# A factorization-machine kernel in fp32 pieces: P5's copy subtracted early from two outputs, P3's halves in two pairs of banks, a split first load, and one more kind of wait on GpSimd

## The chip, the cores and the metric

The kernel runs on one core of a Trainium2 chip. The metric is the device time of one execution in microseconds. Before the change it is 1290.17 us, the median of three runs (1287.72, 1290.17 and 1290.63).

## The reference

x is 1024 x 512, weight 64 x 512 x 512 (embedding, feature, model), lin_w 512 x 512, all float32:

```python
out_lin = x @ lin_w.T + lin_b
xv = jnp.einsum('bf,efm->bem', x, weight)
zp = jnp.einsum('bf,efm->bem', jnp.square(x), jnp.square(weight))
interaction = 0.5 * jnp.sum(jnp.square(xv) - zp, axis=1)
return out_lin + interaction
```

Nearly all the work is xv: 1024 x 512 times 512 x 32768, squared and summed over the 64 embeddings. zp needs only the sum over e of the squared weights, so it is one 512 x 512 product, as the linear layer is.

## The kernel before, in words

**One product in seven parts.** Every 2 x 2 block product is made from seven block products, P1 to P7, in Strassen's manner. x is cut into four blocks (A11, A12, A21, A22) and their sums R5, R6, R7, R3. The weights come in 32 slices `h`, each of four blocks `w11`, `w12`, `w21`, `w22` of 128 x 2 x 512 and sums of them in `T`, which GpSimd's accumulating DMAs make. In every slice the parts run in the order `(1, 6, 2, 3, 7, 5, 4)`, where 5 is that of the next slice.

**fp32 in three pieces.** Each operand is split into pieces H, L and K in the type fp32r; one part is then H times H, L times L and, some matmuls later, K times K (`product`, line 695; two 128 x 512 matmuls for each of H, L and K and each of the four row groups). ScalarE makes H by a scaled copy (line 359), VectorE or GpSimd makes L, GpSimd makes the K of the weights (line 377). The pieces of x (`X1H` to `X7K`) are made once, in `x_pieces`. For x blocks marked "DMA" in `X_SPLIT`, ScalarE writes three scaled copies and two accumulating DMAs, issued by GpSimd, finish L and K; for those marked DVE, VectorE does it in two instructions. The first slice's P1 and P2 are plain fp32 matmuls, as are the linear layer (lines 509 and 520) and the squares (line 520); a plain 128 x 512 matmul has two records in the trace.

**Banks.** PSUM is used as four tiles `bank_0` to `bank_3`, each a pair of 128 x 512 banks. The planner treats a read or write of one half of such a pair as a touch of the whole pair.

**Start.** Two zero matmuls (line 537) run while the first loads come in. A11 and A12 are loaded by SP in halves (`load_x`, line 421), lin_w by ScalarE's queue in four pieces of 256 KB (`load_lw`, line 426, tiles `p5_0` and `p5_1`, shown as `p`). The linear layer's seven parts follow; VectorE makes the column sums `lt1` to `lt4` that its P5, P6, P7 and P4 need (line 371, `p<-p,p`) and then the x sums R5, R7, R6 and R3.

**The plan.** The instructions are not issued in the order of the code. `Plan` simulates the engines with a table of costs, orders each engine's list by due times that are counted back from TensorE's chain, does so 60 times with some due times drawn earlier, and keeps the order that ends first. `landing(name, at)` tells it when a load arrives; `key` sets TensorE's order. VectorE instructions with two SBUF inputs are marked `both`, since GpSimd and VectorE hold each other up there; the planner may let a GpSimd instruction wait, by a semaphore (`o.after`), for such a VectorE instruction.

**End.** After the last slice the squares run as seven parts (`one_level`) into four outputs o(r,c), which have been filled with the linear layer (`lind`) and the accumulated interaction (`accd`). `into` adds or subtracts one bank half from an output half on VectorE, `store` sends a half (256 KB) to HBM. o(0,0) is the tile `p1_0`, o(1,0) `p1_1`, o(1,1) `p5_1`, o(0,1) `p5_2`. P1 and P2 make o(0,0). P5 is copied twice by ScalarE, into `z` and `y` (tiles `w`); P6 and P7 are subtracted from these and the result is subtracted from o(0,1) and o(1,1).

Of the kernel before, what the change touches and what calls it, by code (L numbers as in the profile page):

```python
# [14 lines left out]
AF = mybir.ActivationFunctionType  # L15
# [15 lines left out]
X_SPLIT = {5: DVE, 6: DVE, 3: DVE, 7: DVE, 1: "DMA", 2: "DMA", 4: "DMA"}  # L31
# [10 lines left out]
class Plan:  # L42
# [104 lines left out]
    def forward(self, chain):  # L147
# [62 lines left out]
        while len(done) < len(ops):  # L210
            now = heapq.heappop(times)
            moved = True
            while moved:
                moved = False
                for e in pending:
# [40 lines left out]
def kernel(  # L256
# [24 lines left out]
    nc = tc.nc  # L281
# [8 lines left out]
    H = B // 2  # L290
# [141 lines left out]
    load_x("A11", 0, 3.9)  # L432
# [4 lines left out]
    load_lw(nc.scalar, [0, 1], 1, 7.8)  # L437
    load_x("A12", 1, 8.2)
    load_lw(nc.scalar, [2, 3], 1, 8.8)
    for at, (n, k) in enumerate((("A22", 0), ("A22", 1), ("A21", 0), ("A21", 1))):  # L440
        load_x(n, k, 10.0 + 0.8 * at)
    nc.sync.dma_start(bias[:], lin_b)
    landing("bias", 13.5)
# [96 lines left out]
    plan.add({PE: 3.0}, None, (), tuple(f2), key=-2000)  # L540
# [313 lines left out]

    last = wsquare()
# [9 lines left out]
    def into(n, bank, sub, u):  # L865
        o = buf[n][:, u]
        dve(o, o, buf[bank[u]], sub, ((n, u), bank[u]), ((n, u),))

    def store(r, c, u):
        n = o_name[r, c]  # L870
        dma(out_dst[:, 2 * c + u, ts(r, H)], buf[n, u], ((n, u),), (), 1.0, (SP, ACT))

    f1, f2, f3, f4 = four()
    key = slot[0]
    one_level(1, right, left, f1, True, key)
    one_level(2, right, left, f2, True, key + 2.5)
    for u in range(2):
        into(o_name[0, 0], f1, False, u)
        into(o_name[0, 0], f2, False, u)
        store(0, 0, u)  # L880
    one_level(5, right, left, f3, True, key + 5)
    z, y = kept["w"](), kept["w"]()
    for n in (z, y):
        for u in range(2):
            used((n, u), n)
            act(buf[n, u], buf[f3[u]], AF.Copy, (f3[u],), ((n, u),), 512)
# [5 lines left out]
    one_level(4, right, left, f3, True, key + 11)  # L892
    for u in range(2):
        into(o_name[1, 0], f3, False, u)
    one_level(7, right, left, f1, False, key + 14)
    for u in range(2):
        into(y, f1, False, u)
        n = o_name[1, 1]
        dve(buf[n, u], buf[n, u], buf[y, u], True, ((n, u), (y, u)), ((n, u),), 512, True)
        store(1, 1, u)  # L900
        into(o_name[1, 0], f1, False, u)
        store(1, 0, u)
    one_level(3, right, left, f4, True, key + 17)
    for u in range(2):
        into(o_name[0, 1], f4, True, u)
        store(0, 1, u)
# [43 lines left out]
```

## Time and profile before

| what | before |
|---|---|
| median of 3 runs | 1290.17 us (1287.72 to 1290.63) |
| the profiled execution | 1289.52 us |
| its span, first to last instruction | 1286.7 us |
| TensorE busy | 1277.7 us, 99% of the span |
| VectorE, GpSimd, ScalarE busy | 1221.4, 1047.2, 967.5 us |
| mean granted TensorE clock | 0.999 |
| DMA | 172.96 MB, 134 GB/s |

Around the span lie 1289.52 - 1286.7 = 2.8 us in that execution. In the timeline a row is: start in us, length in us, engine, line, operation, output and inputs, shape, count, and in brackets the idle time of the engine before it with the instruction that ended it. Several neighbouring instructions of one kind are merged into a row. The letters behind the tile names (`w`, `p`, `bank`) stand for all tiles of that family.

### The profile page before, as it was taken

To read this page: it belongs to the slowest core of one execution; us is meant where nothing else is said; L and a number is where in the kernel's file an instruction comes from. 1 tells how busy PE (TensorE), PEld (TensorE's weight loads), DVE (VectorE), ACT (ScalarE), POOL (GpSimd) and SP (SyncE) were. 2 spreads that over 40 slices of the span, in tenths; PEclk is the share of its full clock that TensorE was granted. 3 is DMA by queue.
4 is the path that set the end of the run, shared out by engine and by line. 5 is a ranking of instruction groups with operands and counts; after the bars stand their busy time and mean duration, and the time that the engine had idled before them with its cause. 6 is when DMAs were issued, how large, how long until landed. Compare 5 with 4: busy or idle time off the path is not lost.

```text
span 1286.7 us, 15428 instructions
## 1 busy us (share of the span) xinstructions
PE 1277.7 (99%) x5476; PEld 1024.1 (80%) x5476; DVE 1221.4 (95%) x1016; ACT 967.5 (75%) x1009; POOL 1047.2 (81%) x534
## 2 busy tenths in 40 slices
PE   9999999999999999999999999999999999999998
PEld 4688888888888888888888888888888888888883
DVE  6799999999999999999999999999999999999996
ACT  7578777777787777877777877777778777787781
POOL 2879988888898888898888888888889788889881
PEclk9999999999999999999999999999999999999999
DMA  8886654446654455664445665444665444565456
GB/s 239 189 226 148 145 119 120 99 112 152 147 124 123 103 109 141 152 140 119 106 103 131 148 152 116 119 99 112 151 147 129 119 99 109 143 151 137 129 109 162
DMA packets 68348, 172.96 MB, mean 134 GB/s; under 512 B 22960, under 2 KB 23984, under 8 KB 68272
## 3 DMA queue, kind: packets, MB, share of 16 engines
q0 software_dynamic: 20736, 73.93, 33.4%
q1 hardware_dynamic: 45440, 95.18, 22.4%
q10 hardware_dynamic: 2096, 2.88, 0.6%
q8 instruction: 42, 0.69, 0.2%
q14 instruction: 34, 0.28, 0.1%
HBM read 160.43 MB, written 6.29 MB: 130 GB/s over the span
## 4 chain that ended last, share of the span: by engine, by line
PE 98%; DVE 1%; DMA 0%; ACT 0%; DVEq 0%; issue 0%
PE bank L695 94%; PE bank L520 3%; PE bank L509 1%; DVE X7K L365 0%; DVE p L371 0%; DMA p<-lin_wT 0%; DVE bank L365 0%; DVE X3K L365 0%; DVE w L371 0%; DVE w_sum L384 0%; ACT pH L359 0%; DVEq L946 0%; DVEq L371 0%
## 5 line engine op out<-in xcount | busy, mean ns | idle before, releaser
L377 POOL TENSOR_TENSOR pK<-pH,pL 128x1024 fp32r<-128x1024 f32 x222 | 570.5, 2573 | 154.8 <-PE bank L695 150.2
L359 ACT ACTIVATE sq<-bank 128x1024 f32<-128x1024 f32 x256 | 262.0, 1023 | 97.2 <-issue 47.3
L384 DVE TENSOR_REDUCE acc<-sq 128x16 f32<-128x1024 f32 x256 | 309.0, 1208 | 2.6 <-ACT sq L359 2.6
L377 POOL TENSOR_TENSOR pL<-T,pL 128x1024 fp32r<-128x1024 f32 x96 | 255.3, 2660 | 16.2 <-ACT pL L359 16.2
L365 DVE SCALAR_TENSOR_TENSOR bank<-bank,w 128x1024 f32<-128x1024 f32 x192 | 234.6, 1222 | 0.7 <-PE bank L695 0.6
L371 DVE TENSOR_TENSOR w<-bank,p 128x1024 f32<-128x1024 f32 x128 | 155.8, 1217 | 25.9 <-PE bank L695 25.9
L359 ACT ACTIVATE p<-bank 128x1024 f32<-128x1024 f32 x128 | 130.8, 1023 | 58.7 <-PE bank L695 58.5
L365 DVE SCALAR_TENSOR_TENSOR pL<-pH,w 128x1024 fp32r<-128x1024 f32 x62 | 163.1, 2631 | 0.3 <-ACT pH L359 0.3
L365 DVE SCALAR_TENSOR_TENSOR bank<-bank,p 128x1024 f32<-128x1024 f32 x128 | 153.2, 1218 | 6.6 <-ACT p L359 5.7
L359 ACT ACTIVATE pL<-T 128x1024 fp32r<-128x1024 f32 x96 | 101.3, 1055 | 75.8 <-issue 70.1
L377 POOL TENSOR_TENSOR pL<-w,pL 128x1024 fp32r<-128x1024 f32 x64 | 155.0, 2421 | 2.3 <-ACT pL L359 2.3
L384 DVE TENSOR_REDUCE w_sum<-wsq 128x16 f32<-128x1024 f32 x128 | 154.7, 1209 | 2.1 <-ACT wsq L359 2.1
L359 ACT ACTIVATE pH<-w 128x1024 fp32r<-128x1024 f32 x126 | 133.2, 1057 | 10.6 <-PE bank L695 6.4
L359 ACT ACTIVATE wsq<-w 128x1024 f32<-128x1024 f32 x128 | 134.8, 1053 | 5.0 <-DVE w_sum L384 5.0
L396 POOL DMA_DIRECT2D T<-weight x96 | 92.4, 963 | 36.6 <-DMA T<-weight 17.0
L359 ACT ACTIVATE pH<-T 128x1024 fp32r<-128x1024 f32 x96 | 101.2, 1054 | 0.0
L359 ACT ACTIVATE pL<-w 128x1024 fp32r<-128x1024 f32 x64 | 68.1, 1064 | 40.7 <-PE bank L695 23.6
L695 PE MATMUL bank<-pH,X4H 128*128 128x512 f32 x256 | 81.3, 398 | 0.0
L695 PE MATMUL bank<-pL,X4L 128*128 128x512 f32 x256 | 79.5, 392 | 0.0
L695 PE MATMUL bank<-pH,X5H 128*128 128x512 f32 x256 | 79.2, 391 | 0.0
L695 PE MATMUL bank<-pH,X3H 128*128 128x512 f32 x256 | 79.0, 390 | 0.2 <-DVE w L371 0.2
L695 PE MATMUL bank<-pL,X3L 128*128 128x512 f32 x256 | 78.8, 389 | 0.0
(117 smaller groups left out, 2552.4 us busy)
## 6 DMA issues: line engine op xcount, KB each, us to landing
w<-weight SPq DMA_DIRECT2D x128, 512.0 KB, 5.9
T<-weight POOLq DMA_DIRECT2D x96, 512.0 KB, 6.1
T<-weight SPq DMA_DIRECT2D x32, 512.0 KB, 5.0
w<-weight POOLq DMA_DIRECT2D x32, 512.0 KB, 6.5
accd<-turned SPq DMA_DIRECT2D x64, 32.0 KB, 5.7
p<-lind SPq DMA_DIRECT2D x4, 512.0 KB, 4.2
out<-p ACTq DMA_DIRECT2D x7, 256.0 KB, 2.1
w<-xT SPq DMA_DIRECT2D x6, 256.0 KB, 5.1
```

What stands on the lines that cost most here:

```text
L359: nc.scalar.activation(o, i, func, bias=bias, scale=scale)
L365: return nc.vector.scalar_tensor_tensor(o, i, scalar, j, ALU.mult, op)
L371: return (nc.vector.tensor_sub if sub else nc.vector.tensor_add)(o, a, b)
L377: return (nc.gpsimd.tensor_sub if sub else nc.gpsimd.tensor_add)(o, a, b)
L384: lambda _: nc.vector.tensor_reduce(o, i.rearrange("p a (m e) -> p a m e", e=E), axis=AX.X, op=ALU.add),
L396: {POOL: 0.62}, lambda _: nc.gpsimd.dma_start(o, i, accum_op=ALU.add),
L509: return nc.tensor.matmul(buf[bank[u]], b[:, k, ts(u, P)], a[:, k, :], start=first and k == 0, stop=k == KH - 1, skip_group_check=True,)
L520: made = nc.tensor.matmul(buf[bank[u]], b[:, k, ts(u, P)], a[:, k, :], start=first and k == 0, stop=k == KH - 1, skip_group_check=True,)
L695: made = nc.tensor.matmul(buf[bank, j], buf[x][:, k, ts(2 * half + j, P)], buf[w][:, k, :], start=first and k == 0, stop=k == KH - 1, skip ...
```

## The change

Five edits, of which two act through the planner:

1. X1's pieces L and K come from VectorE (`X_SPLIT[1]` is DVE) and no longer from three ScalarE copies and two accumulating DMAs.
2. The planner adds a semaphore wait where GpSimd starts a compute instruction while, by the plan, a `both` instruction of VectorE is running and none is held back. That is the case when VectorE got its turn because GpSimd's next instruction was a DMA issue.
3. The first lin_w load (256 KB) becomes two of 128 KB. The arrival times that the planner is told are changed; the zero matmuls are planned with 3.4 instead of 3.0 us.
4. The squares at the end: P5 is copied once, into `z`, and that copy is subtracted from o(0,1) and o(1,1) at once; P6, P7 and P3 are subtracted from the outputs directly. P2 comes after the last K parts of the last slice (`key + 4` for `key + 2.5`).
5. P3's two halves go to one half each of two pairs (`f3 = f4[0], f2[0]`), before to the two halves of one pair.

```diff
-X_SPLIT = {5: DVE, 6: DVE, 3: DVE, 7: DVE, 1: "DMA", 2: "DMA", 4: "DMA"}
+X_SPLIT = {5: DVE, 6: DVE, 3: DVE, 7: DVE, 1: DVE, 2: "DMA", 4: "DMA"}
...
                     elif tensor and held is None and free[DVE] > now and running[DVE].both:
+                        o.after = running[DVE]
                         ends(e, o, free[DVE] + cost)
...
-    load_lw(nc.scalar, [0, 1], 0, 3.9)
-    load_x("A11", 1, 5.2)
-    load_lw(nc.scalar, [2, 3], 0, 5.6)
+    load_lw(nc.scalar, [0], 0, 4.3)
+    load_lw(nc.scalar, [1], 0, 5.1)
+    load_x("A11", 1, 5.9)
+    load_lw(nc.scalar, [2, 3], 0, 7.0)
...
-    plan.add({PE: 3.0}, None, (), tuple(f2), key=-2000)
+    plan.add({PE: 3.4}, None, (), tuple(f2), key=-2000)
...
+    def columns(n, m, sub, u):
+        o, i = buf[n][:, u], buf[m][:, u]
+        dve(o, o, i, sub, ((n, u), (m, u)), ((n, u),), 512, True)
+
+    v, f2, f5, f4 = four()
+    f3 = f4[0], f2[0]
+    one_level(1, right, left, v, True, key)
+    one_level(2, right, left, f2, True, key + 4)
...
+    one_level(5, right, left, f5, True, key + 6)
+    z = kept["w"]()
+    for u in range(2):
+        used((z, u), z)
+        act(buf[z, u], buf[f5[u]], AF.Copy, (f5[u],), ((z, u),), 512)
+        for r in range(2):
+            columns(o_name[r, 1], z, True, u)
+    one_level(6, right, left, v, False, key + 8)
+    for u in range(2):
+        into(o_name[0, 1], v, True, u)
...
-    one_level(6, right, left, f1, False, key + 8)
-    for u in range(2):
-        into(z, f1, False, u)
-        n = o_name[0, 1]
-        dve(buf[n, u], buf[n, u], buf[z, u], True, ((n, u), (z, u)), ((n, u),), 512, True)
...
-    one_level(3, right, left, f4, True, key + 17)
+    one_level(7, right, left, v, False, key + 14)
     for u in range(2):
-        into(o_name[0, 1], f4, True, u)
+        into(o_name[1, 1], v, True, u)
+        store(1, 1, u)
+        into(o_name[1, 0], v, False, u)
+        store(1, 0, u)
+    one_level(3, right, left, f3, True, key + 17)
+    for u in range(2):
+        into(o_name[0, 1], f3, True, u)
         store(0, 1, u)
```

The lists of the engines are the same from about the fourth slice to the last one; they differ in about the first hundred instructions of VectorE and ScalarE, the first seventy of GpSimd, and at the end. A line number of the kernel after is one to two (at the end four) higher.

The first place is VectorE's list from its first instruction. `p5_0`, `p5_1` hold lin_w, `p1_1` the column sums `lt1` and `lt2`, `p5_2` the sums `lt3` and `lt4`; `sq_0` is R5, `w_0` R7. Before:

```order
L371 TENSOR_TENSOR p1_1_108<-p5_0_111 128x512
L371 TENSOR_TENSOR p1_1_108<-p1_1_108,p5_1_112 128x512
L371 TENSOR_TENSOR p5_2_113<-p5_0_111,p5_1_112 128x512
L371 TENSOR_TENSOR p5_2_113<-p5_1_112,p1_1_108 128x512
L371 TENSOR_TENSOR sq_0_104<-w22_1_92,p1_0_107 128x1024
L371 TENSOR_TENSOR w_0_109<-w11_1_87,p1_0_107 128x1024
```

After:

```order
L372 TENSOR_TENSOR X1L_66<-w11_1_87,X1H_65 128x1024
L372 TENSOR_TENSOR p1_1_108<-p5_0_111 128x512
L372 TENSOR_TENSOR p1_1_108<-p1_1_108,p5_1_112 128x512
L372 TENSOR_TENSOR p5_2_113<-p5_1_112,p1_1_108 128x512
L372 TENSOR_TENSOR p5_2_113<-p5_0_111,p5_1_112 128x512
L366 SCALAR_TENSOR_TENSOR X1K_67<-X1H_65,X1L_66 128x1024
L372 TENSOR_TENSOR sq_0_104<-w22_1_92,p1_0_107 128x1024
```

X1L stands ahead of the column sums and X1K between them and R5; `lt4`, which P4 reads, comes before `lt3`.

The second place is GpSimd's list in the first slice, with the semaphores that each instruction waits for. `pL_0`, `pK_0` belong to P5 of the first slice, `pL_2` to `w22`. Before:

```order
L377 TENSOR_TENSOR pL_0_98<-T_0_93,pL_0_98 128x1024 [waits DMASW0_49,Activation_49]
L396 DMA T_0_93<-weight 128x1024 [waits Activation_49,Pool_49]
L377 TENSOR_TENSOR pK_0_101<-pH_0_95,pL_0_98 128x1024
L396 DMA w12_0_88<-weight 128x1024 [waits DMAHW0_49,Activation_49]
L377 TENSOR_TENSOR pL_2_100<-w22_0_91,pL_2_100 128x1024 [waits DMAHW2_49,Activation_49]
```

After:

```order
L378 TENSOR_TENSOR pL_0_98<-T_0_93,pL_0_98 128x1024 [waits DMASW0_49,DVE_49,Activation_49]
L397 DMA T_0_93<-weight 128x1024 [waits Activation_49,Pool_49]
L378 TENSOR_TENSOR pK_0_101<-pH_0_95,pL_0_98 128x1024 [waits DVE_49]
L397 DMA w12_0_88<-weight 128x1024 [waits DMAHW2_49,Activation_49]
L378 TENSOR_TENSOR pL_2_100<-w22_0_91,pL_2_100 128x1024 [waits DMAHW3_49,DVE_49,Activation_49]
```

The order is the same; the three compute instructions now wait for VectorE: by the plan for X3L, X3K and X7K. These are the only three waits of this kind that are added in the whole program.

The third place is the end of VectorE's list, from the work on P6 on. `bank_0` holds P1, P6 and P7 in turn, `bank_2` P5 and then P4, `bank_3` P3 (after: `bank_3` and `bank_1`); `wsq_0` is the last part of the interaction. Before:

```order
L365 SCALAR_TENSOR_TENSOR p5_1_112<-wsq_0_106,p5_1_112 128x512
L371 TENSOR_TENSOR w_1_110<-w_1_110,bank_0_114 128x512
L371 TENSOR_TENSOR p1_1_108<-p1_1_108,bank_0_114 128x512
L371 TENSOR_TENSOR p5_1_112<-p5_1_112,w_1_110 128x512
L371 TENSOR_TENSOR w_1_110<-w_1_110,bank_0_114 128x512
L371 TENSOR_TENSOR p5_1_112<-p5_1_112,w_1_110 128x512
L371 TENSOR_TENSOR p5_2_113<-p5_2_113,bank_3_117 128x512
L371 TENSOR_TENSOR p1_1_108<-p1_1_108,bank_0_114 128x512
L371 TENSOR_TENSOR p5_2_113<-p5_2_113,bank_3_117 128x512
```

After:

```order
L372 TENSOR_TENSOR p5_2_113<-p5_2_113,w_0_109 128x512
L372 TENSOR_TENSOR p5_2_113<-p5_2_113,bank_0_114 128x512 x2
L372 TENSOR_TENSOR p1_1_108<-p1_1_108,bank_2_116 128x512
L366 SCALAR_TENSOR_TENSOR p5_1_112<-wsq_0_106,p5_1_112 128x512
L372 TENSOR_TENSOR p1_1_108<-p1_1_108,bank_2_116 128x512
L366 SCALAR_TENSOR_TENSOR p5_2_113<-wsq_0_106,p5_2_113 128x512
L372 TENSOR_TENSOR p5_1_112<-p5_1_112,bank_0_114 128x512
L372 TENSOR_TENSOR p1_1_108<-p1_1_108,bank_0_114 128x512
L372 TENSOR_TENSOR p5_1_112<-p5_1_112,bank_0_114 128x512
L372 TENSOR_TENSOR p5_2_113<-p5_2_113,bank_3_117 128x512
L372 TENSOR_TENSOR p1_1_108<-p1_1_108,bank_0_114 128x512
L372 TENSOR_TENSOR p5_2_113<-p5_2_113,bank_1_115 128x512
```

Before, three instructions stand from P3's first half on, and both P3 rows read one pair, whose matmuls end together; after, P3's first half is alone in `bank_3` and one row stands behind the last matmul. The subtraction of the P5 copy (`w_0`) from o(0,1) now stands ahead of the two rows that take P6 out of `bank_0`, into which P7 is accumulated next.

More of the change, by code (lines that the diff above doesn't have):

```diff
@@ L430, in load_lw @@
             landing((n, z % KH, c), at)
-    load_x("A11", 0, 3.9)
-    load_lw(nc.scalar, [0, 1], 0, 3.9)
-    load_x("A11", 1, 5.2)
-    load_lw(nc.scalar, [2, 3], 0, 5.6)
+    load_x("A11", 0, 4.2)
+    load_lw(nc.scalar, [0], 0, 4.3)
+    load_lw(nc.scalar, [1], 0, 5.1)
+    load_x("A11", 1, 5.9)
+    load_lw(nc.scalar, [2, 3], 0, 7.0)
     load_x("A12", 0, 7.4)
-    load_lw(nc.scalar, [0, 1], 1, 7.8)
-    load_x("A12", 1, 8.2)
-    load_lw(nc.scalar, [2, 3], 1, 8.8)
+    load_lw(nc.scalar, [0, 1], 1, 8.8)
+    load_x("A12", 1, 8.5)
+    load_lw(nc.scalar, [2, 3], 1, 9.6)
     for at, (n, k) in enumerate((("A22", 0), ("A22", 1), ("A21", 0), ("A21", 1))):
-        load_x(n, k, 10.0 + 0.8 * at)
+        load_x(n, k, 10.1 + 0.7 * at)
     nc.sync.dma_start(bias[:], lin_b)
-    landing("bias", 13.5)
+    landing("bias", 12.5)
     nc.scalar.preload_act_table(AF.Square)
@@ L853, with into, store @@
                 dma_add(buf[n, u], acc_dram[:, ch, ts(r, H)], acc_names(ch), ((n, u),), 1.4, 5.0)
+    def into(n, bank, sub, u):
+        o = buf[n][:, u]
+        dve(o, o, buf[bank[u]], sub, ((n, u), bank[u]), ((n, u),))
+    def store(r, c, u):
+        n = o_name[r, c]
+        dma(out_dst[:, 2 * c + u, ts(r, H)], buf[n, u], ((n, u),), (), 1.0, (SP, ACT))
+    def columns(n, m, sub, u):
[3 more added lines that the diff above has]
+    f3 = f4[0], f2[0]
+    key = slot[0]
+    one_level(1, right, left, v, True, key)
+    one_level(2, right, left, f2, True, key + 4)
+    for u in range(2):
+        into(o_name[0, 0], v, False, u)
+        into(o_name[0, 0], f2, False, u)
+        store(0, 0, u)
+    one_level(5, right, left, f5, True, key + 6)
[8 more added lines that the diff above has]
+        into(o_name[0, 1], v, True, u)
+    one_level(4, right, left, f5, True, key + 11)
+    for u in range(2):
+        into(o_name[1, 0], f5, False, u)
     last = wsquare()
```

30 lines of the change are left out of this document (removed).

## The prediction

> **What bounds the kernel now.** I read the page first, then TensorE's waits, then three stretches of the timeline: the start, 24 to 44 us, the end.
>
> ```profile
> PE 1277.7 (99%) x5476; PEld 1024.1 (80%) x5476; DVE 1221.4 (95%) x1016; ACT 967.5 (75%) x1009; POOL 1047.2 (81%) x534
> ...
> PE 98%; DVE 1%; DMA 0%; ACT 0%; DVEq 0%; issue 0%
> ```
>
> The first row is the engines' busy time, the second the chain that ended last: 98% of it is TensorE. The stage table says where the rest can lie (length, then TensorE's busy time):
>
> ```profile
> 40.00:1240.00 1200.00, 1199.75 (x5258) 982.44 (x5257) 1158.33 (x951) 923.33 (x960) 1015.48 (x508) 1.00 0.55 130
> ```
>
> In these 1200 us TensorE misses 0.25 us. The change leaves the matmuls and, but for the last few, their order, so it can touch only what TensorE waits for and what lies before its first and behind its last matmul. TensorE's waits, all of them (total, times, longest):
>
> ```profile
> PE bank L695 <- DVE p L371: 1.4, 1, 1.4
> PE bank L537 <- PEq L939: 0.8, 1, 0.8
> PE bank L509 <- DMA p<-lin_wT: 0.6, 1, 0.6
> PE bank L695 <- DVE w L371: 0.2, 1, 0.2
> ```
>
> So there are four small prizes: 0.6 us at the first real matmul, 1.4 us near 38 us, 0.2 us near 1047 us, and the tail. A change of 0.2% is 2.6 us, about what a measurement of this kernel can tell from none; the total is of that size.
>
> **The first load (edit 3).** Zero matmuls, the linear layer, and when the loads land behind their issue (first line ScalarE's lin_w, second SP's x; min, median, max):
>
> ```profile
> 0.74 2.04 ACTq L426 DMA_DIRECT2D p<-lin_wT  x4
> 0.79 3.75 PE L537 MATMUL bank<-const-float32-0.0 128*128 128x512 f32 x4 [0.79 <-PEq L939]
> 5.16 7.13 PE L509 MATMUL bank<-w,p 128*128 128x512 f32 x16 [0.63 <-DMA p<-lin_wT]
> 5.90 1.06 ACT L359 ACTIVATE X1L<-w 128x1024 fp32r<-128x1024 f32 x1 [1.81 <-DMA w<-xT]
> ```
> ```profile
> DMA to landing us min/median/max: 4.4/6.1/7.1
> ```
> ```profile
> DMA to landing us min/median/max: 3.4/5.1/6.4
> ```
>
> The first lin_w piece lands at 0.74 + 4.4 = 5.14, and TensorE starts at 5.16; the first half of A11 is there by 0.75 + 3.4 = 4.15, and the zero matmuls end at 4.54. With half the bytes ahead the first piece lands earlier by the time of 128 KB:
>
> ```profile
> 3.40:4.40 1.00, 1.00 (x2) 0.00 (x0) 0.00 (x0) 0.70 (x1) 0.00 (x0) 1.00 1.04 343
> ```
>
> At 343 GB/s that is 0.38 us alone and 0.76 us where x takes half. So TensorE starts between 4.54 and 4.76, and gains 0.40 to 0.62; I take 0.6. Next late is A11's second half: it lands by 5.90 (ScalarE's wait above) and is wanted after four records of 0.43 us, at 4.54 + 1.72 = 6.26. Then P4 needs the column sums:
>
> ```profile
> 9.53 1.89 DVE L371 TENSOR_TENSOR p<-p,p 128x512 f32<-128x512 f32 x3
> 12.13 3.60 PE L520 MATMUL bank<-w,p 128*128 128x512 f32 x8
> 12.24 1.23 DVE L371 TENSOR_TENSOR sq<-w,p 128x1024 f32<-128x1024 f32 x1 [0.82 <-DMA p<-xT]
> ```
>
> P4 at 12.13 - 0.6 = 11.5 would just meet the sums' end at 11.42; in the new order the sum that it reads is the third of the four, done at 10.8. X1L runs before 8.80, when VectorE was idle. X1K (1.22 us by X6K's row below) falls into the gap of 0.82 us before R5, so R5 ends 0.4 us later, at 13.9; P5 wants it when P4's eight records of 0.43 us are through, near 15.0. Two ScalarE copies and two GpSimd DMA issues leave the early lists; nothing waited for them. Edit 1 costs nothing here while those 1.1 us hold.
>
> **The stall near 38 us (edit 2).** VectorE, GpSimd and TensorE up to 39 us:
>
> ```profile
> 22.52 1.22 DVE L365 SCALAR_TENSOR_TENSOR X6K<-X6H,X6L 128x1024 fp32r<-128x1024 f32 x1
> ...
> 28.87 1.32 DVE L371 TENSOR_TENSOR p<-p,bank 128x512 f32<-128x512 f32 x2
> 30.10 5.72 DVE L365 SCALAR_TENSOR_TENSOR X7K<-X7H,X7L 128x1024 fp32r<-128x1024 f32 x1
> 35.75 0.68 DVE L371 TENSOR_TENSOR p<-p,bank 128x512 f32<-128x512 f32 x1
> 36.35 1.21 DVE L384 TENSOR_REDUCE w_sum<-wsq 128x16 f32<-128x1024 f32 x1
> 37.48 1.27 DVE L371 TENSOR_TENSOR p<-p,bank 128x512 f32<-128x512 f32 x2
> ```
> ```profile
> 28.79 2.71 POOL L377 TENSOR_TENSOR pK<-pH,pL 128x1024 fp32r<-128x1024 f32 x1
> 31.16 1.17 POOL L396 DMA_DIRECT2D w<-weight  x1
> 31.77 2.96 POOL L377 TENSOR_TENSOR pL<-w,pL 128x1024 fp32r<-128x1024 f32 x1
> ...
> 37.29 2.37 POOL L377 TENSOR_TENSOR pL<-T,pL 128x1024 fp32r<-128x1024 f32 x1 [1.71 <-ACT pL L359]
> ```
> ```profile
> 35.97 1.48 PE L695 MATMUL bank<-pK,X5K 128*128 128x512 f32 x4
> 38.80 3.70 PE L695 MATMUL bank<-w,w 128*128 128x512 f32 x8 [1.35 <-DVE p L371]
> ```
>
> X6K took 1.22 us; X7K, the same instruction, took 5.72, to 35.82, that is 1.1 us past the end of GpSimd's second instruction (31.77 + 2.96 = 34.73). So VectorE waited through two GpSimd instructions with a DMA issue between, and the add that frees TensorE's bank came at 38.75. With the new wait the second GpSimd instruction starts only when X7K is done. X7K then runs from GpSimd's first end, 31.50, to 32.6, 3.2 us earlier, and the last add ends near 35.5. TensorE wants the bank at 38.80 - 1.35 - 0.6 = 36.85, so 1.3 us are to spare and **the 1.35 us go**. Behind the waiting GpSimd instruction stand a DMA issue and the `pL` at 37.29, which was itself idle for 1.71 us until ScalarE had its input; starting 0.9 us later is hidden by that. The two other new waits are for X3L and X3K, which end before or while GpSimd would wait anyway. Where GpSimd's lateness is not hidden it costs up to 0.9 us; I take 0.
>
> [...]
>
> The second wait of this kind, 0.2 us near 1047, follows one such meeting of the two engines. No wait is added there, but the engines meet at other offsets; I count 0.1 us of gain, bounds a loss of 0.4 and a gain of 0.2.
>
> **The tail (edits 4 and 5).** Last rows of TensorE, VectorE and ScalarE's queue:
>
> ```profile
> 1273.68 3.60 PE L520 MATMUL bank<-T,T 128*128 128x512 f32 x8
> 1277.11 3.60 PE L520 MATMUL bank<-w,w_sum 128*128 128x512 f32 x8
> 1278.70 4.32 ACTq L391 DMA_DIRECT2D out<-p  x6
> 1280.74 1.88 DVE L371 TENSOR_TENSOR p<-p,bank 128x512 f32<-128x512 f32 x3 [0.15 <-PE bank L520]
> ```
>
> TensorE ends at 1280.71; three additions of 0.6 us follow and end at 1282.62, then the last store. After, P3's first half is added while the second runs, and one addition of 0.69 us is left: 1.2 us less. The DMA sets the other bound. The first of the six stores is issued at 1278.1 (0.6 earlier, since `y` no longer has to take P7 first); at 343 GB/s one takes 0.76 us, so the five ahead of the last fill the DMA until 1278.1 + 3.8 = 1281.9 on the scale of issues, and the last is issued at 1281.5, 1.2 earlier than now. Up to 0.4 of the 1.2 may stay in that queue; I take a gain of 1.05, bounds 0.6 (the whole queue follows its first store) and 1.2. ScalarE's two copies fewer were on no path. Moving P2 behind both K parts brings the last interaction sums forward by one P2, 3.4 us; they were not waited for.
>
> The new wait is ahead of P7. VectorE now has the addition that needs `accd` in o(0,1) in front of the two that empty `bank_0`, and P7 waits for these. That transfer, its landing behind the issue, and its use before:
>
> ```profile
> 1267.27 0.86 POOL L396 DMA_DIRECT2D p<-accd  x1 [10.05 <-DMA p<-lind]
> ...
> 1271.72 0.68 DVE L371 TENSOR_TENSOR p<-p,w 128x512 f32<-128x512 f32 x1
> ```
> ```profile
> p<-accd POOLq DMA_DIRECT2D x1, 256.0 KB, 4.2
> ```
> ```profile
> p<-accd POOLq DMA_DIRECT2D x3, 256.0 KB, 9.2
> ```
>
> It lands near 1267.3 + 4.2 = 1271.5; three VectorE instructions of 0.6 us then end at 1273.4, and P7 starts at 1273.68. The margin is 0.3 us, and the last `accd` loads now run in the same microseconds. I take a loss of 0.1; bounds 0 and, by the three such transfers that took 9.2 us in a busier stretch, 4.8.
>
> **Sum.** -0.6 - 1.35 - 0.1 - 1.05 + 0.1 = -3.0 us. From the profiled 1289.52 us that gives **1286.5 us**; that execution lies 0.65 below the median of the runs shown, 1290.17, whose runs spread over 2.9 us.
>
> **The rivals.**
>
> *The early start is lost.* The zero matmuls run at half the speed of the linear layer's:
>
> ```profile
> L537 PE MATMUL bank<-const-float32-0.0 x4: 1061/1061/1190, 0.8 to 3.5; 128*128 128x512 f32 x4
> ```
> ```profile
> L509 PE MATMUL bank<-w,p x16: 592/592/697, 5.2 to 11.7; 128*128 128x512 f32 x16
> ```
>
> Somewhere between 4.5 and 5.16 TensorE became fast, while the granted clock reads 1.00 throughout. If that moment stays, matmuls begun at 4.54 do half the work until 5.16 and 0.31 us is lost; if P4 or R5 is late as well, all 0.6: 1286.8 to 1287.1. [...]
>
> *The wait moves instead of going.* GpSimd's lateness passes through its DMA issue to a later piece, or X7K is held up elsewhere, and TensorE stalls 1.35 us anyway: 1287.9. Against it stands GpSimd's idle 1.71 us.
>
> *New meetings.* In the first 110 us, where three lists are reordered, or later by other offsets, VectorE and GpSimd block each other so that two to four stalls of 0.2 to 1.4 us arise, 2 to 3 us in all: 1288.5 to 1289.5. For it: 1.35 and 0.2 arose so. Against: in 30 slices it happened once.
>
> *Slower: P7 waits for the transfer.* If the `accd` addition takes 9.2 us as its three likes did, it lands at 1276.5, P7 starts near 1278.5 instead of 1273.68, and 4.8 us are lost: 1286.5 - 0.1 + 4.8 = 1291.2. Below a landing of 1271.8 this costs nothing, from 1274.7 on it eats the whole gain. Against it: that queue was emptier by 1267.
>
> **How the numbers follow.** The forecast gets 0.60, the lost start 0.12, the moved wait 0.12, new meetings 0.10, the late transfer 0.06. Faster by over 0.2% means below 1287.6: most of the forecast and of the lost start, 0.64 together; slower by over 0.2% means above 1292.7: 0.05; the rest, 0.31, lies between. The forecast's own range is 1284.8 to 1288.2 (bounds of the terms and the spread of the runs). The full range reaches down to 1284.4, all terms at their best (0.62 + 1.35 + 0.2 + 1.2 = 3.4) in a run like the lower ones, and up to 1289.4, the end of the third rival; the late transfer is left out.
>
> **What would show it.** The first row of L509 at 4.5 to 4.8 and its mean length; X7K of some 2.5 us with GpSimd's `pL` behind it, and no wait of TensorE for `p` near 37; P7 following P4 without a gap; one VectorE addition behind the last matmul. A wait of TensorE for VectorE of more than 0.5 us anywhere else, or a tail from the last matmul to the end of the span as long as now (1286.7 - 1280.7 = 6.0 us), would make me wrong.

## The result and the profile after

The kernel after takes **1286.01 us** (median of nine runs, 1284.73 to 1287.37) beside 1290.14 us of the kernel before on the same chip (nine runs, 1287.72 to 1291.21): a ratio of 0.997, 95% interval 0.9960 to 0.9981, so 2.5 to 5.2 us less. The profiled execution took 1285.96 us with a span of 1284.0; that of before had 1289.52 and 1286.7. Of the 3.6 us between these two, 2.7 lie in the span and 0.9 around it. What lies around the span is 1.9 to 2.4 us in nearly all runs of both kernels; the profiled execution of before, with 2.8, is one of the few above (7 of the 70 runs of before whose span is on record).

TensorE's busy time is what it was, and that of the others is within 4 us of it; VectorE has two instructions more, ScalarE four fewer:

```profile
PE 1277.9 (100%) x5476; PEld 1024.1 (80%) x5476; DVE 1224.3 (95%) x1018; ACT 963.9 (75%) x1005; POOL 1043.5 (81%) x532
```

TensorE's waits of before for `p` and `w` by VectorE are gone, and so is that for the first lin_w piece. Two new ones stand there:

```profile
PE bank L522 <- issue: 0.6, 1, 0.6
PE bank L697 <- ACT p L360: 0.3, 1, 0.3
```

**The start.** TensorE, VectorE and ScalarE's queue in the kernel after:

```profile
0.79 3.75 PE L539 MATMUL bank<-const-float32-0.0 128*128 128x512 f32 x4 [0.79 <-PEq L943]
4.33 7.55 PE L511 MATMUL bank<-w,p 128*128 128x512 f32 x16
11.91 3.70 PE L522 MATMUL bank<-w,p 128*128 128x512 f32 x8
```
```profile
9.72 0.69 DVE L372 TENSOR_TENSOR p<-p 128x512 f32<-128x512 f32 x1 [1.44 <-DMA p<-lin_wT]
10.44 2.02 DVE L372 TENSOR_TENSOR p<-p,p 128x512 f32<-128x512 f32 x3
```
```profile
0.74 3.82 ACTq L427 DMA_DIRECT2D p<-lin_wT  x5
```

The real matmuls begin at 4.33, 0.83 us earlier than the 5.16 of before and with no pause behind the zero matmuls. But their sixteen records take 7.55 us where they took 7.13, and P4 begins at 11.91 for 12.13: 0.22 earlier. The fifth lin_w load is issued only near 4.5 (the row of five issues ends at 0.74 + 3.82; the four of before ended at 2.78), the first column sum starts 0.92 later than before, and P4 waits for the sums.

**24 to 44 us.** VectorE and GpSimd, then TensorE and ScalarE:

```profile
26.66 3.06 DVE L366 SCALAR_TENSOR_TENSOR X3K<-X3H,X3L 128x1024 fp32r<-128x1024 f32 x1
...
30.85 2.54 DVE L366 SCALAR_TENSOR_TENSOR X7K<-X7H,X7L 128x1024 fp32r<-128x1024 f32 x1
```
```profile
29.82 2.47 POOL L378 TENSOR_TENSOR pK<-pH,pL 128x1024 fp32r<-128x1024 f32 x1
32.16 0.97 POOL L397 DMA_DIRECT2D w<-weight  x1
33.53 2.36 POOL L378 TENSOR_TENSOR pL<-w,pL 128x1024 fp32r<-128x1024 f32 x1 [0.40 <-issue]
```
```profile
35.89 1.48 PE L697 MATMUL bank<-pK,X5K 128*128 128x512 f32 x4
37.22 3.59 PE L697 MATMUL bank<-w,w 128*128 128x512 f32 x8
...
43.87 0.73 PE L697 MATMUL bank<-pH,X6H 128*128 128x512 f32 x2 [0.33 <-ACT p L360]
```
```profile
40.90 1.06 ACT L360 ACTIVATE pL<-w 128x1024 fp32r<-128x1024 f32 x1 [0.89 <-DMA w<-weight]
41.86 1.05 ACT L360 ACTIVATE pH<-w 128x1024 fp32r<-128x1024 f32 x1
42.81 1.01 ACT L360 ACTIVATE p<-bank 128x1024 f32<-128x1024 f32 x1
```

X7K takes 2.54 us for 5.72, GpSimd's next `pL` starts behind it at 33.53, and the plain matmuls follow at 37.22 (38.80 before) with no wait. Six microseconds later TensorE waits for a ScalarE copy (`p<-bank`) that starts at 42.81, behind two instructions on `w12`, the first of which waited for the accumulating transfer.

**The end.** TensorE, VectorE, GpSimd's last transfer and the stores:

```profile
1268.38 3.60 PE L522 MATMUL bank<-w,T 128*128 128x512 f32 x8
1272.57 3.67 PE L522 MATMUL bank<-T,T 128*128 128x512 f32 x8 [0.59 <-issue]
1276.08 3.60 PE L522 MATMUL bank<-w,w_sum 128*128 128x512 f32 x8
```
```profile
1270.39 0.69 DVE L372 TENSOR_TENSOR p<-p,w 128x512 f32<-128x512 f32 x1 [2.13 <-DMA p<-accd]
1271.18 1.88 DVE L372 TENSOR_TENSOR p<-p,bank 128x512 f32<-128x512 f32 x3
...
1279.71 0.69 DVE L372 TENSOR_TENSOR p<-p,bank 128x512 f32<-128x512 f32 x1 [0.35 <-PE bank L522]
```
```profile
1266.01 0.86 POOL L397 DMA_DIRECT2D p<-accd  x1 [10.70 <-DMA p<-lind]
```
```profile
1277.00 3.77 ACTq L392 DMA_DIRECT2D out<-p  x6
```

P7 (`T,T`) starts 0.6 us after P4's end (1268.38 + 3.60 = 1271.98). VectorE waited 2.13 us for `accd`, and behind that addition stand the two that empty P7's bank, until about 1272.5; run 5 tests that this is the cause. One addition stands behind the last matmul, which ends at 1279.68; from there to the end of the span it is 4.3 us, 6.0 before.

The ledger of the two profiled executions, from the start of one and the same matmul in both (before and after, us):

| up to | before | after | sum so far | step |
|---|---|---|---|---|
| first real matmul | 5.16 | 4.33 | -0.83 | -0.83 |
| P5 of the linear layer | 15.56 | 15.45 | -0.11 | +0.72, given back |
| plain matmuls after the stall | 38.80 | 37.22 | -1.58 | -1.47 |
| the wait for ScalarE | 45.34 | 44.20 | -1.13 | +0.45 |
| slices up to 933 us | 933.25 | 931.66 | -1.60 | -0.47, in small pieces |
| past the waits at 1047 and 1083 | 1115.67 | 1113.83 | -1.84 | -0.24 |
| P7's second record | 1274.11 | 1273.08 | -1.03 | +0.81 |
| end of the span | 1286.69 | 1284.00 | -2.69 | -1.66 |

### The profile page after: what moved, and what is told of

It reads as the page before. It is cut to its first block, busy times and chain, and to the rows that moved or that the text cites. A ratio compares the mean times of both kernels' runs of the same rounds, so it can differ in the third digit from the quotient of the medians.

```text
span 1284.0 us, 15422 instructions
## 1 busy us (share of the span) xinstructions
PE 1277.9 (100%) x5476; PEld 1024.1 (80%) x5476; DVE 1224.3 (95%) x1018; ACT 963.9 (75%) x1005; POOL 1043.5 (81%) x532
## 4 chain that ended last, share of the span: by engine, by line
PE 94%; DVE 3%; DMA 2%; ACT 0%; issue 0%; ACTq 0%; SPq 0%; DVEq 0%
PE bank L697 92%; PE bank L522 2%; DMA w<-weight 1%; DMA p<-lin_wT 1%; DVE pL L366 0%; DVE bank L366 0%; DVE acc L385 0%; DVE X3K L366 0%; DVE p L372 0%; DVE w L372 0%; ACT pH L360 0%; ACT sq L360 0%; ACTq L427 0%; DVE X7K L366 0%; DVE sq L366 0%
## 5 line engine op out<-in xcount | busy, mean ns | idle before, releaser
L366 DVE SCALAR_TENSOR_TENSOR pL<-pH,w 128x1024 fp32r<-128x1024 f32 x62 | 167.4, 2700 | 0.0
L697 PE MATMUL bank<-pH,X6H 128*128 128x512 f32 x256 | 78.9, 389 | 0.3 <-ACT p L360 0.3
```

What stands on the lines that cost most here:

```text
L366: return nc.vector.scalar_tensor_tensor(o, i, scalar, j, ALU.mult, op)
L697: made = nc.tensor.matmul(buf[bank, j], buf[x][:, k, ts(2 * half + j, P)], buf[w][:, k, :], start=first and k == 0, stop=k == KH - 1, skip ...
```

## The experiments

Theory after the result: three separate gains (the wait, the tail, something at the start) and two losses that the change brings itself (near 43.5 us and ahead of P7). Rivals: that one of the gains is only the shadow of another, and that the losses have other causes. All kernels ran beside the kernel before on their chip; edit 1 was not tried by itself.

**1. The wait alone,** in the kernel before:

```diff
+                        o.after = running[DVE]
```

> The kernel before with the one line of edit 2 and nothing else; the lists of all engines stay those of before, three GpSimd instructions get a wait for VectorE. Theory A (the stall near 38 us came from X7K being blocked through two GpSimd instructions, and the wait removes it whole): X7K takes about 2.5 us, TensorE's wait of 1.35 us for p is gone, no new wait of TensorE near 43 us, since in this kernel X3L (ends 24.88) and X3K (ends 28.95) are through when GpSimd's pL (25.51) and pK (28.79) want to start; 1.3 to 1.5 us less than the kernel before. Theory B (the waits for X3L and X3K make GpSimd late whatever the rest, and the lateness passes through the DMA issue behind them to w12's accumulating transfer): a stall of 0.5 to 0.7 us near 43 us appears here as it does in the kernel after; 0.8 us less than before. Theory C (the wait saves nothing, the stall went by X1's new place): no difference, TensorE still waits 1.35 us near 38 us.

1287.49 us median (12 runs) beside 1289.46; ratio 0.9987 (0.9977 to 0.9998). TensorE's only wait for another engine or a transfer, and VectorE's X7K:

```profile
PE bank L510 <- DMA p<-lin_wT: 1.3, 1, 1.3
```
```profile
30.41 2.50 DVE L366 SCALAR_TENSOR_TENSOR X7K<-X7H,X7L 128x1024 fp32r<-128x1024 f32 x1
```

Theory A: no wait near 38 us and none near 43. The gain is edit 2's own; its size in the runs, 0.3 to 3.0 us by the interval, is less sharp than the trace.

**2. The tail alone,** edits 4 and 5 in the kernel before, as in the diff of the change.

> The kernel before with edits 4 and 5 (the squares at the end) and nothing else; all lists are those of before until the last slice. Theory A (the tail behind the last matmul gets 1.7 us shorter and P7 waits 0.8 us for bank_0, because an addition that needs the accd transfer stands ahead of the two that empty it): 0.9 us less than before, last matmul to end of span 4.3 us for 6.0, a gap between P4 and P7 of 0.7 to 0.9 us. Theory B (the wait of P7 in the kernel after came from the earlier parts of the change, which brought the end forward against the transfers): no gap, 1.0 to 1.7 us less. Theory C (the tail is paid for in full by the stores' queue): tail as long as before, 0 to 0.8 us more.

1287.35 us (11 runs) beside the same 1289.46; ratio 0.9987 (0.9977 to 0.9996). The tail behind the last matmul is 4.5 us, and P7 is late here as well:

```profile
PE bank L695 <- DVE p L371: 1.3, 1, 1.3
...
PE bank L520 <- issue: 0.3, 1, 0.3
```

The last row is P7's; the old stall is still there. Theory A for the mechanism, with a gap ahead of P7 of 0.92 us between records that are 0.43 apart elsewhere; the runs are 2.1 us faster in the median, 0.5 to 3.0 by the interval, which can't tell A's 0.9 from B's 1.0 to 1.7.

**3. The kernel after without the wait.**

```diff
-                        o.after = running[DVE]
```

> The kernel after without the line of edit 2: lists as in the kernel after, the three waits gone. Theory A (the wait is worth the old stall less what it makes late): X7K is blocked through two GpSimd instructions again (above 5 us), TensorE waits 1.3 to 1.6 us near 38 us, and the stall near 43 us is gone; 0.8 to 1.0 us more than the kernel after, about 3.2 us less than before. Theory B (with X1 on VectorE the two engines meet at other offsets, so that X7K is not caught and the wait was not needed): as fast as the kernel after or up to 0.6 us faster. Theory C (X3K is caught as well): two stalls, 2 us or more above the kernel after.

1289.84 us median beside 1289.46, ratio 1.0016 (0.9993 to 1.0039), but from 1286.57 to 1298.79 (12 runs): five runs lie above 1296. One of these is the profiled one, VectorE, GpSimd, TensorE:

```profile
31.94 13.61 DVE L365 SCALAR_TENSOR_TENSOR X7K<-X7H,X7L 128x1024 fp32r<-128x1024 f32 x1
```
```profile
30.67 2.73 POOL L377 TENSOR_TENSOR pK<-pH,pL 128x1024 fp32r<-128x1024 f32 x1
33.05 1.18 POOL L396 DMA_DIRECT2D w<-weight  x1
33.66 2.97 POOL L377 TENSOR_TENSOR pL<-w,pL 128x1024 fp32r<-128x1024 f32 x1
35.97 1.50 POOL L396 DMA_DIRECT2D T<-weight  x1
36.58 3.29 POOL L377 TENSOR_TENSOR pL<-T,pL 128x1024 fp32r<-128x1024 f32 x1
38.92 5.53 POOL L377 TENSOR_TENSOR pK<-pH,pL 128x1024 fp32r<-128x1024 f32 x2
51.73 2.37 POOL L377 TENSOR_TENSOR pL<-w,pL 128x1024 fp32r<-128x1024 f32 x1 [7.28 <-ACT pL L359]
```
```profile
48.52 5.09 PE L696 MATMUL bank<-w,w 128*128 128x512 f32 x8 [9.79 <-DVE p L371]
```

No theory had this. X7K waits through five GpSimd instructions and two DMA issues and ends at 45.55, 1.1 us after GpSimd runs out of work at 44.45; TensorE stands for 9.8 us. It then runs eight records in 5.09 us instead of 3.6: the granted clock, 0.996 in this run, is at one half up to 51.36. Here and in the profile of before (34.73 and 35.82) X7K ends 1.1 us after GpSimd's last unbroken instruction, so in both its length is that of GpSimd's unbroken work. In the order of before that is nearly the same each time (TensorE waits 1.35, 1.3 and 1.3 us in the profiles of before, run 2 and run 10, and none of 79 runs of before is above 1292.61); the long stall belongs to the order with X1 on VectorE. That the other four runs above 1296 have it too wasn't seen, as one only was profiled.

**4. Only the third wait,** that for X7K:

```diff
+        met = 0
...
-                        o.after = running[DVE]
+                        met += 1
+                        o.after = running[DVE] if met == 3 else None
```

> The kernel after with only the third of the three new waits (pL_2 of w22 for X7K); pL and pK of the first slice no longer wait for X3L and X3K. Theory A (these two waits made GpSimd 0.8 to 1.0 us late, its DMA issue for w12 followed as late, and ScalarE's copy and TensorE near 43.5 us behind it): pL starts at about 25.4 instead of 26.3, the w12 issue about 0.8 earlier, TensorE's wait of 0.6 us near 43.5 is gone, X7K still takes about 2.5 us; 0.5 to 0.6 us less than the kernel after. Theory B (w12's late landing comes from its load, which SP issues behind lind in the new order): the stall near 43.5 stays, same time as the kernel after. Theory C (without the waits X3K is caught by both GpSimd instructions, and the stall of 1.4 us comes back by that way): 0.5 to 1.5 us more than the kernel after.

1285.52 us (6 runs) beside 1289.46; ratio 0.9966 (0.9954 to 0.9978). GpSimd's `pL` starts at 25.46 (26.29 after), and no wait is seen near 43.5. That looked like theory A; run 8 took it back.

**5. P7 freed of the transfer.**

```diff
-        for r in range(2):
-            columns(o_name[r, 1], z, True, u)
+        columns(o_name[1, 1], z, True, u)
...
-        into(o_name[0, 1], v, True, u)
+        into(z, v, False, u)
+        columns(o_name[0, 1], z, True, u)
```

> The kernel after with P6 added to the copy of P5 (tile w, after that copy has been subtracted from o(1,1)), and the copy then subtracted from o(0,1); so nothing that empties bank_0 ahead of P7 needs the accd transfer into o(0,1). As many VectorE instructions as after. Theory A (P7 waited for that transfer): the gap between P4's last matmul and P7 (1.19 us after, 0.92 and 0.68 in the two other kernels with this tail) is 0.43, the tail behind the last matmul stays 4.3 to 4.5 us; 0.3 to 0.8 us less than the kernel after, about 4.7 less than before. Theory B (the addition in front waits for another transfer, that into o(1,1), just as long): the gap stays above 0.6 us, same time as after. Theory C (o(0,1) becomes late at the end, since its chain is now one step longer): gap gone, tail longer by as much.

1285.06 us (6 runs) beside 1289.88; ratio 0.9966 (0.9954 to 0.9978). P4 and P7 follow each other at 3.44 us, and the tail is 4.35:

```profile
1267.91 3.60 PE L522 MATMUL bank<-w,T 128*128 128x512 f32 x8
1271.35 3.60 PE L522 MATMUL bank<-T,T 128*128 128x512 f32 x8
```

Theory A for the mechanism. Its median is 1.0 us below those of runs 7 and 8 beside it, which the intervals don't separate.

**6. One first load again.**

```diff
-    load_lw(nc.scalar, [0], 0, 4.3)
-    load_lw(nc.scalar, [1], 0, 5.1)
+    nc.scalar.dma_start(buf["lw0"][:, 0:KH, ts(0, HM)], lw_src[:, 0:KH, ts(0, HM)])
+    landing(("lw0", 0, 0), 4.3)
+    landing(("lw0", 1, 0), 5.1)
```

> The kernel after with the first two lin_w loads of 128 KB put back into one of 256 KB, the planner told the same arrivals: all lists as after but for that load. Theory A (the earlier start is eaten up at once, by half-speed matmuls at the beginning and by the last lin_w piece, which as the ninth load waits for the first to land): first real matmul at 5.1 to 5.3, the first column sum about 0.9 earlier than after (8.8 for 9.72), no gap before P4, X5H's first matmul within 0.3 us of the kernel after's 28.78; the time within 0.5 us of the kernel after. Theory B (the earlier start is worth its 0.6 us): 0.6 us more than the kernel after, X5H at 29.4 or later. The moment from which matmuls run at full speed differs from run to run by up to 4 us of the start, so the comparison is made on the runs' medians and in the trace by the gaps.

1286.80 us (11 runs, 1285.23 to 1289.40) beside 1289.88; ratio 0.9983 (0.9973 to 0.9992), 0.7 to 1.7 us above the three kernels of this comparison with the split load. Theory B by size, but not by its reason. The sixteen matmul records of the linear layer's P1 and P2 (shortest, median and longest in ns, first and last start), here, in the tail alone (run 2), in the kernel after, and in the same kernel run again (run 12):

```profile
L512 PE MATMUL bank<-w,p x16: 592/592/1221, 5.2 to 13.5; 128*128 128x512 f32 x16
```
```profile
L509 PE MATMUL bank<-w,p x16: 592/592/1222, 5.2 to 13.7; 128*128 128x512 f32 x16
```
```profile
L511 PE MATMUL bank<-w,p x16: 592/592/1101, 4.3 to 11.3; 128*128 128x512 f32 x16
```
```profile
L511 PE MATMUL bank<-w,p x16: 592/592/697, 4.5 to 11.1; 128*128 128x512 f32 x16
```

From the first to the last start it is 8.3 and 8.5 us in the first two, 7.0 and 6.5 in the others, and 6.5 in the profile of before. In the first two the records start 0.85 us apart instead of 0.43 up to 8.8 us. Where the first start is 5.2, TensorE has paused for 0.9 us behind the zero matmuls; so it has in the profile of before, which came out of it at full speed, as run 1 did after a still longer one (sixteen records in 7.13 us).

**7. A12 in one load,** so that the fifth lin_w load needn't wait:

```diff
-    load_x("A12", 0, 7.4)
+    nc.sync.dma_start(buf["A12"][:], x_src[:, KH:NK, ts(0, H)])
+    landing(("A12", 0), 7.4)
...
-    load_x("A12", 1, 8.5)
+    landing(("A12", 1), 8.5)
```

> The kernel after with A12's two halves in one load of 512 KB, the planner told the same arrivals: with eight loads at the start the last lin_w piece no longer waits for the first load to land; all lists as after otherwise. Theory A (the late piece held up the column sums and they P4): the fifth lin_w issue at about 2.5 instead of 4.5 us, the first column sum below 9.2 (9.72 after), no gap between P2 and P4; 0.2 to 0.4 us less than after. Theory B (the piece is late by its share of the transfers, not by its issue): sums as late as after, same time. Theory C (A12 as one load lands too late for P2's first matmuls): a gap before P2 near 7.9 us, 0.2 to 1 us more.

1286.11 us (6 runs) beside 1289.88; ratio 0.9972 (0.9960 to 0.9983). The issue came at 3.2 at the latest, and still the sums got later:

```profile
9.06 0.69 DVE L372 TENSOR_TENSOR p<-p 128x512 f32<-128x512 f32 x1 [0.72 <-DMA p<-lin_wT]
11.28 2.02 DVE L372 TENSOR_TENSOR p<-p,p 128x512 f32<-128x512 f32 x3 [1.52 <-DMA p<-lin_wT]
```

Theory B: with the earlier issue the last three sums still end later (13.30 for 12.46), so the issue alone doesn't set them. That it is the share of the transfers is argued, since A12 came as one load of twice the size as well. P4 waited 1.06 us.

**8. P3 in one pair** (edit 5 undone).

```diff
-    f3 = f4[0], f2[0]
+    f3 = f4
```

> The kernel after with edit 5 undone: P3's two halves in the two halves of one pair of banks, all else as after but the place of one VectorE row and one store. Theory A (the addition of the first half waits for all of P3, so two of the last additions stand behind the last matmul): two to three VectorE rows behind the last matmul, the tail 4.9 to 5.6 us instead of 4.3; 0.6 to 1.2 us more than the kernel after. Theory B (the stores' queue sets the end, as the lower bound of the prediction had it): tail 4.3 to 4.7 us, at most 0.4 us more. Theory C (the whole gain of the tail came from edit 4): same time as after.

1286.06 us (7 runs) beside 1289.88; ratio 0.9973 (0.9962 to 0.9984). Its last rows of VectorE and of the stores:

```profile
1278.69 1.28 DVE L372 TENSOR_TENSOR p<-p,bank 128x512 f32<-128x512 f32 x2 [0.95 <-PE bank L522]
```
```profile
1275.98 4.37 ACTq L392 DMA_DIRECT2D out<-p  x6
```

Two additions behind the last matmul, and the tail is 4.6 us: not theory A. Whether the 0.3 us over the kernel after's 4.3 are edit 5's (B) or nothing (C) isn't shown: in the profiles with edit 5 the tail lies between 4.3 and 4.6 as well (4.6 in run 6). From the end of the last issue to the end of the span it is 3.67 us before (1283.02 to 1286.69), 3.23 after (1280.77 to 1284.00) and 2.91 here (1280.35 to 1283.26).

**9. Both repairs together** (runs 4 and 5).

> The kernel after with two repairs that were each measured alone: only the third GpSimd wait (for X7K), and P6 added to the copy of P5 so that P7 doesn't wait for the accd transfer. Theory A (the stall of 0.6 us near 43.5 and the gap ahead of P7 of 0.3 to 0.8 us are separate and both go): no gap of TensorE above 0.4 us between 13 us and the end but those at the start of a K part that other kernels have too; 0.9 to 1.3 us less than the kernel after run beside it, 5 us less than before. Theory B (after the first repair the transfers at the end come at another time, so that the second brings nothing): 0.5 us less than after.

1285.12 us (5 runs, 1284.60 to 1286.05) beside 1289.46; ratio 0.9964 (0.9951 to 0.9976), while the kernel after in the same comparison (run 12) had 1285.10. No gain that these runs show. P7 waits no more, but the wait for ScalarE is back with only the third wait in the program:

```profile
PE bank L699 <- ACT p L362: 0.3, 1, 0.3
```

So the waits for X3L and X3K aren't its cause, or not alone. What the profiles with it have in common is an early TensorE: its first X6H matmul starts at 41.57 after and at 41.02 here (and at 41.18 in run 12, which lost 0.2 us); without it, at 41.63 (run 4), 41.73 (5) and 41.91 (8), the last two with all three waits. ScalarE's copy starts between 41.9 and 42.8 in all of them.

**10. Before, the pause filled.**

```diff
+    nc.tensor.matmul(
+        buf[f2[0]][:, 0:N // 2], zero[:, 0:P], zero[:, 0:N // 2], start=True, stop=True,
+        skip_group_check=True,
+    )
```

> The kernel before with a third zero matmul of half width, two records of 0.43 us at half speed, which end near 5.19 and so fill the time in which TensorE waits for the first lin_w piece (4.33 to 5.16); nothing else. Theory A (a pause of TensorE just before the real matmuls makes the clock go up late, near 9 us instead of near 5, in about half of the executions; that is why the runs of before lie in two heaps 2.3 us apart, and edit 3 gains by having no pause): the upper heap is gone, all runs between 1287.5 and 1289.5, median 1 to 2 us less than before. Theory B (when the clock goes up has nothing to do with that pause; edit 3 gains by its earlier start): two heaps as before, median within 0.4 us of before.

1288.49 us (11 runs, 1287.97 to 1289.69) beside 1289.46 (21 runs, 1287.65 to 1291.00, eight of them above 1289.7); ratio 0.9995 (0.9986 to 1.0004). None of the eleven is above 1289.7, which speaks for theory A; two lie just below, above A's 1289.5, and the median is 1.0 us lower. That the kernel is faster isn't shown by the interval.

**11. After, with a pause.**

```diff
-            buf[f2[u]], zero[:, 0:P], zero, start=True, stop=True, skip_group_check=True
+            buf[f2[u]][:, 0:N // (1 + u)], zero[:, 0:P], zero[:, 0:N // (1 + u)], start=True,
+            stop=True, skip_group_check=True,
```

> The kernel after with its second zero matmul cut to half width, so that the zero matmuls end at 3.48 instead of 4.33 us and TensorE pauses 0.85 us before the real ones begin at 4.3 to 4.8; nothing else. Theory A (the pause makes the clock go up late): half-speed matmuls until 7 to 10 us in half or more of the executions, an upper heap of runs 2 us above the others, median 0.8 to 2 us more than the kernel after run beside it. Theory B (the pause is of no account): the same as after.

1286.92 us (11 runs, 1285.66 to 1289.60) beside 1289.46; ratio 0.9981 (0.9972 to 0.9990), 1.8 us in the median above run 12, which differs only in that zero matmul:

```profile
L511 PE MATMUL bank<-w,p x16: 592/592/1219, 4.4 to 13.5; 128*128 128x512 f32 x16
```

9.1 us for the sixteen starts: half speed up to 9.6 us. Theory A, though the intervals of the two kernels still touch.

**12. The kernel after again.**

> The kernel after, unchanged, beside the three others for comparison on one chip. By all theories 1285.5 to 1286.5 us median, 3.5 to 4.2 us less than before; where matmuls reach full speed varies between 4.3 and 7 us from run to run, and the gap ahead of P7 lies between 0.6 and 1.4 us.

1285.10 us (5 runs, 1284.45 to 1286.53); ratio 0.9964 (0.9952 to 0.9977). P7 waited longest here:

```profile
1267.88 3.60 PE L522 MATMUL bank<-w,T 128*128 128x512 f32 x8
1273.03 3.67 PE L522 MATMUL bank<-T,T 128*128 128x512 f32 x8 [1.55 <-issue]
```

## Why the prediction was right, and where its terms were not

The forecast of 1286.5 met 1286.0, and the sign and the mechanism of the two main gains, the stall and the tail, were those of the text. That the number came out so close is partly luck. The -3.0 us were taken from an execution with 0.8 us more around its span than usual; from the median of 1290.17 the same sum gives 1287.2. And five terms (the start, the wait for ScalarE, the small pieces, P7 and the tail) were off by about 0.5 to 0.7 us each, two of them left out of the sum, and they largely cancel. One of the text's own signs of being wrong was there, too: P7 did not follow P4 without a gap but came 0.8 us late, held by additions of VectorE, where the text had set 0.5 us as the bound. Term by term:

**The stall near 38 us (-1.35).** Right in mechanism and size: -1.47 in the pair, and with the wait alone 1.7 us by its ratio (0.3 to 3.0). What was too small was the picture of it: "VectorE waited through two GpSimd instructions" was read as the mechanism, and in run 3 X7K took 13.61 us, through five GpSimd instructions, and ended 1.1 us after GpSimd ran out of work at 44.45. In the profile of before two were all that GpSimd had in a row, and X7K took 5.72 us.

**"The two other new waits are for X3L and X3K, which end before or while GpSimd would wait anyway."** Wrong: X1's two instructions push X3L back to 24.93 (23.66 before), and `pL` starts at 26.29 for 25.51. But it cost nothing that can be shown: the loss near 43.5 us, which the rival "the wait moves instead of going" seemed to name, comes with and without these waits. By the profiles it is the next thing that is late once TensorE is early, ScalarE's copy; no run tried that by itself. Whether the transfer of `w12` or ScalarE's own list sets that copy differs between profiles (a wait for the transfer of 0.89 us after, none in run 9); that stays open.

**The first load (-0.6).** The step "TensorE starts between 4.54 and 4.76, and gains 0.40 to 0.62" gave the wrong reason for a gain of about the right size. The start came at 4.33, and the rival had the rest of the profiled pair right: a half-speed record ate 0.36 of the 0.83 us, and the wait for the late sums with the slower record behind it most of 0.36 more. In that pair the start brought 0.11 us. Over many runs it brings more: undoing the split (run 6) or putting a pause back (run 11) costs 0.7 to 1.8 us in the medians. There the gain is the pause that is gone. With it, the real matmuls run at full speed from their start near 5 us or only from near 9 on (run 2, run 6, run 11), and the 30 runs of before beside runs 1 to 4 lie in two groups, 15 from 1287.66 to 1288.98 and 15 from 1289.95 up; without it, all 14 runs of the kernel after lie between 1284.45 and 1287.37.

The granted clock of the profile doesn't show this: it reads 1.00 at the start only because the trace's clock records begin with the first one at full clock. That first record begins at 4.63 us in the profile of before and 3.77 in run 1, at 9.12, 8.81 and 9.60 in runs 2, 6 and 11, and between 3.78 and 6.98 in the other nine profiles. The pause was 0.91, 0.87 and 1.05 us in runs 2, 6 and 11, 0.84 in the profile of before and some 1.5 in run 1 (an estimate from the records' starts, with 0.85 us for each at half speed and 0.43 at full). In the last two the clock had come up before the real matmuls began (5.16 and 5.47), and their sixteen records took 7.13 us in both; in the other three they ran at half speed for 3.6 to 5.2 us. What decides between the two isn't shown: the length of the pause alone doesn't.

**The tail (-1.05, bounds 0.6 to 1.2).** -1.66, outside the bounds, and the reason is the step on the stores: "up to 0.4 of the 1.2 may stay in that queue". The queue got shorter instead. The last issue came 1.2 us earlier against the last matmul, as worked out, and the span then ended 3.23 us behind it for 3.67. The first of the six stores starts 2.7 us before the last matmul's end instead of 2.0, which would explain that, but it wasn't tried by itself. Run 8 parts the two edits: without edit 5 the tail is 4.6 of 6.0 us, so edit 4 brings some 1.4. The other 0.3 can't be put down to edit 5: profiles that have it end between 4.3 and 4.6 us behind the last matmul.

**P7 (+0.1, bounds 0 to 4.8).** The wait was named and under-priced: 0.6 to 0.8 us in the pair; over the nine profiles with this order P7 starts 0 to 1.7 us late (run 8 and run 12). The transfer's 4.2 us were right: it was issued at 1266.0 instead of 1267.3 and used at 1270.4. But TensorE had come forward by 1.8 us, and the text had set the landing against P7's old start. Run 5 shows the cause by removing it.

**1047 us (-0.1).** -0.24 with the wait at 1083 that took its place.

**The sum.** -0.11 - 1.47 + 0.45 - 0.47 - 0.24 + 0.81 - 1.66 = -2.69 in the span of the pair, for the -3.0 forecast: what the tail and the small pieces gave beyond it, the start, ScalarE's copy and P7 took back. In the medians it is 4.1 us. That fits the late clock, which the profile of before happened not to show: eight of the nine runs of before beside the kernel after took 1289.97 us or more, as the upper group does. Where a kernel's runs fall into two groups and its profile shows the late clock, the profiled run is in the upper one (runs 2 and 6), and where it shows the early clock, in the lower (run 1).

## What to carry to other kernels

Before a short wait is priced from one profile, ask what draws its length: here 1.35 us was the wait of one order of the lists, and the same pair of engines waited 9.8 us in another; and about half of the runs carried 2 us at the start that the profile didn't hold. When a stall is removed, write down the next row that is late by less than the gain, on each engine and at each transfer; two of them took back 1.3 us here. And when additions are moved out of a tail, look at what each of them needs: one that needs a transfer, put ahead of those that empty a bank, handed the transfer's lateness to TensorE here, up to 1.7 us of it (run 12).

## What the runs showed of the hardware

X7K, a VectorE instruction with two SBUF inputs, met a running GpSimd instruction in run 1, before and in run 3. It was held until GpSimd paused, in the last two past the end of the instruction that it had met. It ended 1.1 us after the pause began (31.82 and 32.91 us in run 1, 34.73 and 35.82 before, 44.45 and 45.55 in run 3) and so took 2.5, 5.7 and 13.6 us; X6K, the same instruction, took 1.22 with GpSimd idle (before, 22.52). The 0.27 us between two GpSimd instructions in the kernel before (31.50 to 31.77), with a DMA issue in them, did not let X7K in. The issue itself doesn't keep it out: in the kernel after X7K's last 1.1 us, 32.29 to 33.39, lie beside one (32.16 to 33.13).

With a pause of TensorE of 0.8 to 1.5 us ahead of the real matmuls, which then began at 4.4 to 5.5 us, full speed came only at 8.8 to 9.6 us in three of the five profiles that have it (runs 2, 6 and 11); in the other two it came before the pause was over (4.63 before, 3.77 in run 1), and in the nine with a shorter one or none between 3.8 and 7.0. With a matmul on zeros in the pause, none of eleven runs lies above 1289.7, where eight of 21 without it do. In run 3, with the stall of 9.8 us up to 48.52, the granted clock was one half from 41.12 to 51.36.
